# Three of six transformed rows of a 3x3 convolution by F(2,3) along the columns, and six half images' statistics by ScalarE's accumulators

## The chip, the cores and the metric

The kernel runs on one core of a Trainium2 chip. The metric is device time in microseconds (us) from the first to the last instruction of one execution; lower is better. Before the change it is 2940.79 us, the median of three runs from 2938.74 to 2942.02. The profile comes from one further execution with the hardware profiler on.

The engines are TensorE (PE, matmuls; PEld is its weight load, which overlaps), VectorE (DVE), ScalarE (ACT), GpSimd (POOL) and SyncE (SP, which issues DMAs). Each runs its own instructions in a fixed order; an instruction that waits holds up all that stand behind it on its engine. All data is float32.

## The reference

Two layers over `x` of shape (4, 1024, 56, 56). Layer 0 is a bottleneck with a deformable 3x3 convolution (bilinear samples at learned offsets). Layer 1 is a bottleneck with batch norms, whose means and variances run over all four images. The change lies for the most part in layer 1's 3x3 convolution and in the statistics of its output:

```python
x = relu(x + conv1x1(relu(deform_conv3x3(relu(conv1x1(x))))))            # layer 0
out = relu(bn(conv1x1(x, w1, b1), g1, be1))      # 1024 -> 256 channels
out = relu(bn(conv3x3(out, w2, b2), g2, be2))    # 256 -> 256, padding 1
out = bn(conv1x1(out, w3, b3), g3, be3)          # 256 -> 1024
x = relu(x + softplus(residual_scale)[0] * out)
```

## The kernel before

Channels lie on the 128 partitions, 256 of them as two blocks (KB = 2). The kernel has four stages, told apart here by their time in the profiled execution.

1. Layer 0 and layer 1's first 1x1 convolution, 0 to 2145 us. POOL gathers samples, ACT and DVE weight them, PE turns and multiplies them; positions (`stage_b`: o, oi, fl, hi, lo, each with two buffers) are worked out by DVE. In the last image, `filters()` transforms layer 1's 3x3 weights on DVE in pieces, one piece at two of nine taps, and `raw_rows` loads the first rows.
2. Layer 1's 3x3 convolution, 2145 to 2489 us. Below called the column stage.
3. The second norm with its ReLU (L977), and the third norm's statistics out of a matrix of second moments (L947, L966), up to about 2620 us.
4. The last 1x1 convolution, residual and output, to the end.

The column stage works on eight half images (`parts`), each 28 rows of 56 columns. Along the rows it is a Winograd transform F(4,3): groups of four output rows come out of six transformed rows p = 0 to 5 (`v[p]`, seven groups in a half image), with transformed filters `u[p]` that still have three column taps. Along the columns each transformed row is a filter of three taps. It is done with even and odd columns apart: `v[p]` holds the columns as two halves, `vs[p]` their difference, and `us[p]` is the sum of two taps. With these a row p takes five products in place of six. A product is four matmuls (two output blocks by two input blocks) of 196 columns (7 groups x 28), or 203 where one more column is needed; a matmul takes one 128x128 block of weights.

For a row p, `begin` issues eight matmuls into the bank `q` and four into `b`; ACT copies both out (L840, L841) into the rows `TARGET[p]` of the output `y2`, odd and even columns; DVE adds `b` to the odd ones (L844). `end` issues eight more matmuls into `q`, and DVE subtracts them from the even columns (L861). The rows are taken in the order `SEQ` = 1, 2, 3, 4, 0, 5. `end` of p = 2 and p = 4 also carries the inverse transform along the rows on DVE (L869 to L879, its last line writes row 1 of each group, which is the last reader of row 3 before p = 5 is copied there), `end` of 0 and 5 closes it (L883, L886), and `bn_stats` (L866) reads every finished row, eight times 392 elements in a half image.

The inputs of the next half image are made on the way: `load` takes the raw rows by DMA, and ACT normalizes them into one buffer `rows` (L744, four instructions of 784 to 812 elements), which DVE must have finished reading; the last reader is the input of p = 5 (L780, L781), the first user of the new rows is the input of p = 1 and 2 (L770 to L776). `inputs` computes `v[p]` and `vs[p]` (L783) on DVE.

The loop over (half image, p) issues `begin(i, p)`, then `end` of the row before, then inputs of the next half image, then `load` once for each half image. A scheduler may shift instructions on their engine from there, so the order is the one that stands in the built program.

PSUM has eight banks: three `q` of two banks, one `b` of two.

Of the kernel before, what the change touches and what calls it, by code (L numbers as in the profile page):

```python
# [8 lines left out]
F32 = mybir.dt.float32  # L9
I32 = mybir.dt.int32  # L10
AF = mybir.ActivationFunctionType
ALU = mybir.AluOpType
# [17 lines left out]
SEQ = (1, 2, 3, 4, 0, 5)  # L30
TARGET = (0, 0, 1, 2, 3, 3)

SIZES = (512, 512, 512, 512, 384, 384, 320)
# [25 lines left out]
def deform_bottleneck_then_bn_bottleneck(  # L59
# [48 lines left out]
    nc.vector.memset(eps_t, EPS)  # L108
    y1_stats = const.tile([128, KB, NB, 6], F32, tag="y1_stats", name="y1_stats")
    y2_stats = const.tile([128, KB, N * HW // PIECE, 6], F32, tag="y2_stats", name="y2_stats")  # L110

    def scale_shift(stats, k, g, be, name):

        mv = const.tile([128, k, 2], F32, tag=f"mv_{name}", name=f"mv_{name}")
        for i in range(k):
            nc.vector.bn_aggr(mv[:, i, :], stats[:, i, :, :].rearrange("p b s -> p (b s)"))
        return scale_shift_of(mv[:, :, 0], mv[:, :, 1], k, g, be, name)
# [43 lines left out]
    l1 = ExitStack()  # L161
    u, first_rows = [], []

    with ExitStack() as l0:
# [56 lines left out]

        zero = wp.tile([PW + 2, CB], F32, tag="zero", name="zero")
        nc.vector.memset(zero, 0.0)
        def load_zeros():
            for n in range(N):
                for corner, s in enumerate((0, PW)):
                    first_row = PW - s + TPAD
                    for r0, r1 in ((0, first_row), (first_row + H * PW, TROWS)):
                        if r1 > r0:
                            nc.sync.dma_start(tables[n][r0:r1, corner, :], zero[: r1 - r0, :])  # L230
# [109 lines left out]
        def stage_b(n, j):  # L340
# [16 lines left out]
            shape = [128, NT, TAPS, 2]  # L357
            o = work.tile(shape, F32, tag="o", name=f"o_{n}_{j}")[:, :nt]
            oi = work.tile(shape, I32, tag="oi", name=f"oi_{n}_{j}")[:, :nt]
            fl = work.tile(shape, F32, tag="fl", name=f"fl_{n}_{j}")[:, :nt]  # L360
            hi = work.tile(shape, F32, tag="hi", name=f"hi_{n}_{j}")[:, :nt]
            lo = work.tile(shape, F32, tag="lo", name=f"lo_{n}_{j}")[:, :nt]

# [102 lines left out]
        def stage_c(n, j):  # L466
# [56 lines left out]
            for h in range(KB):  # L523
                y1 = w3p.tile([128, 512], F32, tag="x1t", name=f"y1_{b}_{h}", bufs=X1S)
                y1 = y1[:, :size]
                nc.scalar.activation(y1, acc3[:, h, :size], AF.Identity, bias=col("b1", h))
                nc.vector.bn_stats(y1_stats[:, h, b, :], y1)
                nc.sync.dma_start(y1_v[n, :, h, blk], y1)
# [6 lines left out]
        def filters():  # L535
# [34 lines left out]
            yield  # L570
            nc.vector.tensor_scalar_mul(w_0, w_0, 0.25)
            yield

# [65 lines left out]
        for i, (n, j, k) in enumerate(taps):  # L639
# [10 lines left out]
            if (n, j, k) == (N - 1, 1, 0):  # L650
                l0a.close()
                extra = filters()
            if extra and k in (3, 7):
                next(extra, None)
# [28 lines left out]
    with l1:  # L683

        psq = l1.enter_context(tc.tile_pool(name="psq", bufs=3, space=bass.MemoryType.PSUM))
        psb = l1.enter_context(tc.tile_pool(name="psb", bufs=1, space=bass.MemoryType.PSUM))
        wino = l1.enter_context(tc.tile_pool(name="wino", bufs=1))

        stt = nc.vector.scalar_tensor_tensor


        v, vs = [], []
        for p in range(6):
            t = wino.tile([128, QUADS, KB, PW], F32, tag=f"v{p}", name=f"v{p}")
            for side in (0, PW - 1):
                nc.gpsimd.memset(t[:, :, :, side : side + 1], 0.0)
            v.append(t)
            vs.append(wino.tile([128, QUADS, KB, PW // 2], F32, tag=f"vs{p}", name=f"vs{p}"))

        us = [  # L700
            wino.tile([128, KB, CB], F32, tag=f"us{p}", name=f"us{p}") for p in range(6)
        ]
        sum_t = wino.tile([128, KB, QUADS, W], F32, tag="sum_t", name="sum_t")
# [49 lines left out]
        def inputs(i, d, ps):  # L753

            for hs in [slice(h, h + 1) for h in range(KB)] if i == 0 else [slice(0, KB)]:

# [7 lines left out]
                if len(ps) == 2:  # L764
                    p, q = ps
                    x = of(q)
                    y = wino.tile([128, QUADS, KB, W], F32, tag="y", name=f"y{p}_{i}_{hs.start}")
                    y = y[:, :, hs]
                    if p == 1:
# [7 lines left out]
                else:  # L777
# [3 lines left out]
                    stt(of(p), row(r), 4.0, of(p), ALU.mult, ALU.add)  # L781
                for p in ps:
                    stt(  # L783
                        vs[p][:, :, hs], v[p][:, :, hs, : PW // 2], -1.0, v[p][:, :, hs, PW // 2 :],
                        ALU.mult, ALU.subtract,
                    )


# [9 lines left out]

        def taps_of(ps, p, o, terms, start, stop):
            of = slice(o * 128, (o + 1) * 128)  # L800
            terms = [(wt[:, h, of], x[:, :, h]) for h in range(KB) for wt, x in terms]
            for i, (wt, x) in enumerate(terms):
                nc.tensor.matmul(  # L803
                    ps,
                    wt,
                    x,
                    start=start and i == 0,
                    stop=stop and i == len(terms) - 1,

                    skip_group_check=not (start and stop),  # L810
                )

        def cells(t, width):
            return t[:, :, : QUADS * width].rearrange("p o (r c) -> p o r c", c=width)

        def begin(i, p):

            n, half = parts[i]
            at = f"{p}_{i}"
            to = rows_of(n, half, TARGET[p])  # L820
            even, odd = to[:, :, :, 0:W:2], to[:, :, :, 1:W:2]
            x0, x1 = v[p][:, :, :, : PW // 2], v[p][:, :, :, PW // 2 :]
            pq = psq.tile([128, KB, 512], F32, tag="q", name=f"q{at}")
            for o in range(KB):
                taps_of(
                    pq[:, o, : QUADS * half_w], p, o,
                    [(u[p][:, :, c], x1[:, :, :, c // 2 : c // 2 + half_w]) for c in (0, 2)],
                    True, False,
                )
            pb = psb.tile([128, KB, 512], F32, tag="b", name=f"b{at}")  # L830
            for o in range(KB):
                taps_of(
                    pb[:, o, : QUADS * (half_w + 1)], p, o,
                    [(u[p][:, :, 1], x0)], True, True,
                )
            q, b = cells(pq, half_w), cells(pb, half_w + 1)
            for o in [slice(o, o + 1) for o in range(KB)] if p == 1 else [slice(0, KB)]:

                bias = col("b2", o.start) if p == 1 else 0.0
                nc.scalar.activation(odd[:, o], q[:, o], AF.Identity, bias=bias)  # L840
                nc.scalar.activation(  # L841
                    even[:, o], b[:, o, :, :half_w], AF.Identity, bias=bias, scale=-1.0
                )
            nc.vector.tensor_add(odd, odd, b[:, :, :, 1:])  # L844
            return pq

        def end(i, p, pq):

            n, half = parts[i]
            for o in range(KB):  # L850
                taps_of(
                    pq[:, o, : QUADS * half_w], p, o,
                    [
                        (us[p], vs[p][:, :, :, :half_w]),
                        (u[p][:, :, 2], vs[p][:, :, :, 1 : 1 + half_w]),
                    ],
                    False, True,
                )
            r = [rows_of(n, half, k) for k in range(4)]
            even = r[TARGET[p]][:, :, :, 0:W:2]  # L860
            nc.vector.tensor_sub(even, even, cells(pq, half_w))  # L861

            def stats(k):
                b = i * 4 + k
                for o in range(KB):
                    nc.vector.bn_stats(y2_stats[:, o, b, :], r[k][:, o])  # L866

# [17 lines left out]
            elif p == 5:  # L885
                nc.vector.tensor_add(r[3], r[3], far_t)  # L886
                stats(3)

        ds = {0: load(0)}
        for ps in ((1, 2), (3, 4), (0,), (5,)):  # L890
            inputs(0, ds[0], ps)
            for p in ps:
                nc.vector.tensor_add(us[p], u[p][:, :, 0], u[p][:, :, 1])
        before = None
        for i, p in [(i, p) for i in range(len(parts)) for p in SEQ] + [(len(parts), None)]:
            begun = begin(i, p) if p is not None else None
            if before is not None:
                j, q, _ = before
                end(*before)
                if j + 1 < len(parts) and q in (2, 4, 0, 5):  # L900
                    inputs(j + 1, ds[j + 1], (q - 1, q) if q in (2, 4) else (q,))
            if p == SEQ[0] and i + 1 < len(parts):
                ds[i + 1] = load(i + 1)
# [244 lines left out]
```

## Time and profile before

| | |
|---|---|
| median of three runs | 2940.79 us (2938.74 to 2942.02) |
| the profiled execution | 2943.16 us, its span 2941.3 us |
| PE busy | 2878.5 us (98%), 10665 matmuls |
| DVE busy | 1872.9 us (64%) |
| ACT busy | 1143.8 us (39%) |
| POOL busy | 1009.5 us (34%) |
| mean granted TensorE clock | 0.992 |

By stage, from the busy time of each engine in stretches of the span:

| stretch (us) | length | PE | DVE | ACT |
|---|---|---|---|---|
| 1900 to 2050, layer 0 | 150.0 | 150.00 | 103.26 | 64.45 |
| 2157 to 2486, column stage | 329.0 | 327.69 | 261.18 | 82.98 |
| 2486 to 2497, its end | 11.0 | 3.43 | 7.36 | 5.19 |
| 2497 to 2620, second moments | 123.0 | 123.00 | 46.85 | 41.74 |
| 2620 to 2941, output | 321.0 | 316.98 | 145.11 | 145.33 |

A mean duration counts one instruction from its start to its end. Two neighbours on DVE overlap by some 0.08 us where nothing is waited for, so the distance from start to start is shorter than the mean: 0.48 us for 392 elements whose mean is 0.56. Sums below use that distance.

### The profile page before, as it was taken

What the parts mean: (1) busy time and instruction counts of PE and PEld (TensorE: products, weight loads), DVE (VectorE), ACT (ScalarE), POOL (GpSimd) and SP (SyncE); (2) the same over time, 40 slices, a digit from 0 to 9 for tenths busy, and PEclk for the clock granted to TensorE, in tenths of its full rate; (3) what the DMA queues carried; (4) which work ended last, traced back from release to release, by engine and by line L of the source; (5) the groups of instructions that cost most, each with busy time, mean ns of one, the idle gap of its engine ahead of it and who ended that gap; (6) DMA issues with size and microseconds to landing.
All of it is one profiled execution on the core that took longest, in us unless ns stands there. A gap on an engine that the chain in (4) does not pass through costs nothing.

```text
span 2941.3 us, 34573 instructions
## 1 busy us (share of the span) xinstructions
PE 2878.5 (98%) x10665; PEld 1730.7 (59%) x10665; DVE 1872.9 (64%) x4234; ACT 1143.8 (39%) x2343; POOL 1009.5 (34%) x977
## 2 busy tenths in 40 slices
PE   8899999999999999999999899999989998999999
PEld 4444455565555555555555455455689998965554
DVE  2188666676666677566666867667477786344444
ACT  1144443444443444433433344444332222334444
POOL 0065554455455455454454654444100000000000
PEclk9999999999999999999999999999999999999999
DMA  7699999898998998989897899998521101049998
GB/s 250 198 375 382 329 328 321 298 354 319 325 339 313 342 288 336 333 323 343 324 322 268 319 336 330 333 320 299 184 75 46 46 23 54 25 148 316 303 308 263
DMA packets 330329, 789.48 MB, mean 268 GB/s; under 512 B 31352, under 2 KB 176800, under 8 KB 329888
## 3 DMA queue, kind: packets, MB, share of 16 engines
q0 software_dynamic: 127296, 462.48, 44.3%
q1 hardware_dynamic: 172368, 273.41, 27.7%
q10 hardware_dynamic: 30480, 51.39, 4.8%
q8 instruction: 84, 1.38, 0.2%
q14 instruction: 101, 0.83, 0.1%
HBM read 639.11 MB, written 142.70 MB: 266 GB/s over the span
## 4 chain that ended last, share of the span: by engine, by line
PE 90%; DMA 5%; DVE 2%; issue 1%; ACT 1%; SPq 0%; POOL 0%; DVEq 0%; ACTq 0%; POOLq 0%
PE acc L451 23%; PE pf L916 11%; PE acc L262 11%; PE pr L503 10%; PE acc L476 10%; PE q L803 9%; PE stp L435 6%; DMA g<-table,idxs 3%; PE acc_g L966 2%; PE b L803 2%; PE pm L288 2%; DVE s L413 2%; DMA xr<-in_x_dram 1%; PE ftp L318 1%; PE tp L947 1%
## 5 line engine op out<-in xcount | busy, mean ns | idle before, releaser
L401 POOL DMA_INDIRECT g<-table,idxs x900 | 1001.6, 1113 | 1086.7 <-DVE s L413 533.8
L413 DVE SCALAR_TENSOR_TENSOR s<-g,wts,s 128x256 f32<-128x256 f32 (+1 forms) x2700 | 1133.8, 479 | 353.1 <-ACT s L411 227.5
L451 PE MATMUL acc<-sts,w 128*128 128x512 f32 (+2 forms) x2016 | 809.8, 543 | 1.1 <-issue 0.8
L411 ACT ACTIVATE s<-g,wts 128x256 f32<-128x256 f32 x900 | 418.5, 509 | 459.6 <-PE stp L435 342.6
L451 PEld LDWEIGHTS acc<-sts,w 128*128 128x128 f32 x2016 | 363.1, 191 | 283.4 <-issue 201.1
L503 PE MATMUL pr<-r,w 128*128 128x512 f32 (+2 forms) x896 | 368.9, 543 | 7.1 <-ACT sts L441 3.5
L476 PE MATMUL acc<-x1t,c1w 128*128 128x512 f32 (+2 forms) x896 | 368.0, 539 | 5.2 <-ACT x1t L513 4.3
L262 PE MATMUL acc<-xt,w 128*128 128x448 f32 x896 | 354.5, 546 | 13.1 <-DMA xt<-in_x_dram 8.6
L916 PE MATMUL pf<-y,c3w 128*128 128x448 f32 x844 | 317.4, 539 | 0.0
L513 ACT ACTIVATE x1t<-x1t 128x512 f32<-128x512 f32 (+2 forms) x224 | 128.7, 575 | 439.2 <-DVE x1t L510 398.3
L435 PEld LDWEIGHTS stp<-ident,s 128*128 128x128 f32 (+1 forms) x1800 | 212.0, 141 | 138.9 <-issue 89.3
L510 DVE SCALAR_TENSOR_TENSOR x1t<-pr,ch,xr 128x512 f32<-128x512 f32 (+2 forms) x224 | 152.0, 681 | 214.7 <-PE pr L503 148.0
L262 PEld LDWEIGHTS acc<-xt,w 128*128 128x128 f32 x896 | 170.0, 192 | 173.0 <-issue 161.3
L476 PEld LDWEIGHTS acc<-x1t,c1w 128*128 128x128 f32 x896 | 170.0, 190 | 170.0 <-issue 117.7
L503 PEld LDWEIGHTS pr<-r,w 128*128 128x128 f32 x896 | 169.8, 191 | 165.9 <-issue 105.4
L441 ACT COPY sts<-stp 128x512 f32<-128x512 f32 (+2 forms) x504 | 243.1, 526 | 36.1 <-PE stp L435 22.1
L435 PE MATMUL stp<-ident,s 128*128 128x128 f32 (+1 forms) x1800 | 246.2, 273 | 9.9 <-DVE x1t L510 4.9
L1080 DVE SCALAR_TENSOR_TENSOR x1f<-pf,sc_bn,x1f 128x448 f32<-128x448 f32 x211 | 144.3, 684 | 172.3 <-PE pf L916 155.7
L916 PEld LDWEIGHTS pf<-y,c3w 128*128 128x128 f32 x844 | 160.4, 190 | 156.8 <-issue 118.4
L1088 ACT ACTIVATE x1f<-x1f,sh_bn 128x448 f32<-128x448 f32 x224 | 148.2, 667 | 173.8 <-DVE x1f L1080 172.1
L803 PE MATMUL q<-v,u 128*128 128x196 f32 x768 | 140.7, 335 | 9.6 <-DVE v L775 9.6
L803 PEld LDWEIGHTS q<-v,u 128*128 128x128 f32 x768 | 133.2, 191 | 10.5 <-ACT y L744 10.1
(174 smaller groups left out, 1713.3 us busy)
## 6 DMA issues: line engine op xcount, KB each, us to landing
xt<-in_x_dram SPq DMA_DIRECT2D x112, 448.0 KB
x1f<-x_d SPq DMA_DIRECT2D x112, 448.0 KB
out_dram<-x1f ACTq DMA_DIRECT2D x111, 448.0 KB
xr<-in_x_dram SPq DMA_DIRECT2D x64, 512.0 KB
x_d<-x1t SPq DMA_DIRECT2D x128, 256.0 KB
table<-ft SPq DMA_DIRECT2D x56, 384.0 KB
g<-table,idxs POOLq DMA_INDIRECT x900
xr<-in_x_dram SPq DMA_DIRECT2D x32, 384.0 KB
```

What stands on the lines that cost most here:

```text
L262: nc.tensor.matmul(acc[:, h, :BLK], w1[:, k, h * 128 : (h + 1) * 128], xt[:, k % 2, :], start=(k == 0), stop=(k == KC - 1),)
L401: nc.gpsimd.indirect_dma_start(out=g[:m], out_offset=None, in_=tables[n].rearrange("r q c -> r (q c)"), in_offset=bass.IndirectOffsetOnAxi ...
L411: nc.scalar.activation(s[:m], g[:m, 0:CB], AF.Copy, scale=wt[:, 0])
L413: nc.vector.scalar_tensor_tensor(s[:m], g[:m, corner * CB : (corner + 1) * CB], wt[:, corner], s[:m], ALU.mult, ALU.add,)
L435: nc.tensor.transpose(banks[h][:, t * 128 : t * 128 + m], s[:m, h * 128 : (h + 1) * 128], ident[:m, :m],)
L441: nc.scalar.copy(sts[:, h, :size], banks[h][:, :size])
L451: nc.tensor.matmul(acc[:, o, :size], w2[:, h, k, o * 128 : (o + 1) * 128], sts[:, h, :size], start=(k == 0 and h == 0), stop=(k == TAPS - ...
L476: nc.tensor.matmul(acc3[:, h, :size], c1w[:, k, h * 128 : (h + 1) * 128], x1t, start=(k == 0), stop=(k == KC - 1),)
L503: nc.tensor.matmul(pr, w3[:, h, k * 128 : (k + 1) * 128], r2[:, h, :size], start=(h == 0), stop=(h == KB - 1),)
L510: nc.vector.scalar_tensor_tensor(x1t, pr, col("a_b3", k), xr[:, d, :], ALU.add, ALU.add)
L803: nc.tensor.matmul(ps, wt, x, start=start and i == 0, stop=stop and i == len(terms) - 1,  skip_group_check=not (start and stop),)
L916: nc.tensor.matmul(pz, c3w[:, h, k * 128 : (k + 1) * 128], y2[n][:, h, j * BLK : (j + 1) * BLK], start=(h == 0), stop=(h == KB - 1),)
```

## The change

Rows p = 2, 4 and 5 (`WIN`) take another column transform: F(2,3), four products for two output columns. Its weights are made by `column_filters`: (w0 + w2 + w1)/2 goes over tap 1, (w0 + w2 - w1)/2 into `us[p]`; those of p = 2 and 4 (`EARLY`) are made in layer 0, as six more pieces of `filters()`, which now advances at three of nine taps. Its inputs take three DVE instructions for each p: a sum and a difference of the halves into `vs[p]`, now 56 columns wide, and a difference in place, whose column 0 POOL must have set to zero. `begin` now issues four matmuls into `q`, ACT copies -2 times that into the odd columns; a new step `middle` adds four more, and ACT copies the sum into the even columns; `end` adds four into `q` and four into a `b` of their own; DVE adds `q` to the odd and subtracts `b` from the even columns. `q` and `b` are one bank each, with four buffers each.

`bn_stats` stays for the first and the last half image. The six between are read by ACT (`passes`): two halves of each channel block, each with Identity and with Square, 784 elements, less the first half image's mean, with the sum from the accumulator; `gather` makes one entry of them for `bn_aggr`. The passes of a half image stand among the steps of the next one.

The intermediate `y` of `inputs` takes the place of `vs[q]`. The position tiles o, oi, fl, hi, lo have one buffer each; the zero tile for the tables' borders is taken from the ring of the samples' tiles.

```diff
+WIN = (2, 4, 5)
+EARLY = (2, 4)
...
-    y2_stats = const.tile([128, KB, N * HW // PIECE, 6], F32, tag="y2_stats", name="y2_stats")
+    y1_stats = const.tile([128, KB, NB * 6], F32, tag="y1_stats", name="y1_stats")
+
+    y2_stats = const.tile([128, KB, 3 + 2 * 4 * 6], F32, tag="y2_stats", name="y2_stats")
...
-            o = work.tile(shape, F32, tag="o", name=f"o_{n}_{j}")[:, :nt]
-            oi = work.tile(shape, I32, tag="oi", name=f"oi_{n}_{j}")[:, :nt]
-            fl = work.tile(shape, F32, tag="fl", name=f"fl_{n}_{j}")[:, :nt]
-            hi = work.tile(shape, F32, tag="hi", name=f"hi_{n}_{j}")[:, :nt]
-            lo = work.tile(shape, F32, tag="lo", name=f"lo_{n}_{j}")[:, :nt]
+            o = work.tile(shape, F32, tag="o", name=f"o_{n}_{j}", bufs=1)[:, :nt]
+            oi = work.tile(shape, I32, tag="oi", name=f"oi_{n}_{j}", bufs=1)[:, :nt]
+            fl = work.tile(shape, F32, tag="fl", name=f"fl_{n}_{j}", bufs=1)[:, :nt]
+            hi = work.tile(shape, F32, tag="hi", name=f"hi_{n}_{j}", bufs=1)[:, :nt]
+            lo = work.tile(shape, F32, tag="lo", name=f"lo_{n}_{j}", bufs=1)[:, :nt]
...
+            for p in EARLY:
+                us[p] = pool.tile([128, KB, CB], F32, tag=f"us{p}", name=f"us{p}")
+                yield from column_filters(p)
+
+        def column_filters(p):
+
+            w_0, w_1, w_2 = (u[p][:, :, j] for j in range(3))
+            nc.vector.tensor_add(us[p], w_0, w_2)
+            yield
+            nc.vector.tensor_add(w_1, w_1, us[p])
+            nc.vector.tensor_scalar_mul(w_1, w_1, 0.5)
+            yield
+            nc.vector.tensor_sub(us[p], us[p], w_1)
...
-            if extra and k in (3, 7):
+            if extra and k in (1, 4, 7):
...
-        psq = l1.enter_context(tc.tile_pool(name="psq", bufs=3, space=bass.MemoryType.PSUM))
-        psb = l1.enter_context(tc.tile_pool(name="psb", bufs=1, space=bass.MemoryType.PSUM))
+        psq = l1.enter_context(tc.tile_pool(name="psq", bufs=4, space=bass.MemoryType.PSUM))
+        psb = l1.enter_context(tc.tile_pool(name="psb", bufs=4, space=bass.MemoryType.PSUM))
...
+            half_c = PW // 2
+            for p in ps:
+                if p in WIN and i:
+                    nc.gpsimd.memset(v[p][:, :, :, 0:1], 0.0)
...
-                    y = wino.tile([128, QUADS, KB, W], F32, tag="y", name=f"y{p}_{i}_{hs.start}")
-                    y = y[:, :, hs]
+
+                    y = vs[q][:, :, hs]
...
+                    if p in WIN:
+                        x0, x1 = v[p][:, :, hs, 1:half_c], v[p][:, :, hs, half_c : 2 * half_c - 1]
+                        nc.vector.tensor_add(vs[p][:, :, hs, : W // 2], x1, x0)
+                        nc.vector.tensor_sub(vs[p][:, :, hs, W // 2 :], x0, x1)
+                        x = v[p][:, :, hs].rearrange("p r h (e c) -> p r h e c", e=2)
+                        to, nxt = x[..., : half_c - 1], x[..., 1:]
+                        nc.vector.tensor_sub(to, nxt, to)
+                        continue
...
+        def products(ps, terms, first=False, last=False, alone=False):
+
+            for o in range(KB):
+                of = slice(o * 128, (o + 1) * 128)
+                pairs = [(wt[:, h, of], x[:, :, h]) for h in range(KB) for wt, x in terms]
+                for j, (wt, x) in enumerate(pairs):
+                    nc.tensor.matmul(
+                        ps[:, o].rearrange("p r c -> p (r c)"),
+                        wt,
+                        x,
+                        start=first and j == 0 and (alone or o == 0),
+                        stop=last and j == len(pairs) - 1,
+                        skip_group_check=not alone,
...
+                products(q, [(us[p], vs[p][..., half_w:])], first=True)
+                nc.scalar.activation(odd, q, AF.Copy, scale=-2.0)
+                return q
...
+        def middle(i, p, q):
+            if p in WIN:
+                even, _ = halves(i, p)
+                products(q, [(u[p][:, :, 1], vs[p][..., :half_w])])
+                nc.scalar.copy(even, q)
...
+                x0, x1 = v[p][..., :half_w], v[p][..., PW // 2 : PW // 2 + half_w]
+                products(q, [(u[p][:, :, 2], x1)], last=True)
+                b = bank(psb, "b", i, p, half_w)
+                products(b, [(u[p][:, :, 0], x0)], first=True, last=True, alone=True)
+                nc.vector.tensor_add(odd, odd, q)
...
+                if i in ENDS:
+                    for o in range(KB):
+                        at = 3 + (ENDS.index(i) * 4 + k) * 6
+                        nc.vector.bn_stats(y2_stats[:, o, at : at + 6], r[k][:, o])
...
+        def passes(i):
+            n, half = parts[i]
+            size = HALF * W // CUTS
+            for o in range(KB):
+                for c in range(CUTS):
+                    at = half * HALF * W + c * size
+                    k = (i - 1) * CUTS + c
+                    for f, func in enumerate((AF.Identity, AF.Square)):
+                        nc.scalar.activation(
+                            passed,
+                            y2[n][:, o, at : at + size],
+                            func,
+                            bias=away[:, o : o + 1],
+                            accum_out=moved[:, f, o, k : k + 1],
+                        )
+                        yield
...
+        def gather():
+            count = float(between * HALF * W)
+            whole = y2_stats[:, :, 0:3]
+            nc.vector.tensor_reduce(in_sum, moved, mybir.AxisListType.X, ALU.add)
+            nc.vector.memset(whole[:, :, 0], count)
+            stt(whole[:, :, 1], in_sum[:, 0], 1.0 / count, mv_0[:, :, 0], ALU.mult, ALU.add)
+            nc.vector.tensor_mul(in_sum[:, 0], in_sum[:, 0], in_sum[:, 0])
+            stt(
+                whole[:, :, 2], in_sum[:, 0], -1.0 / count, in_sum[:, 1], ALU.mult, ALU.add
+            )
...
+                if q == SEQ[-1]:
+                    if j == 0:
+                        reference()
+                    elif j not in ENDS:
+                        passing = passes(j)
+                for _ in range(2):
+                    next(passing, None)
+                if (j, q) == (len(parts) - 1, SEQ[-2]):
+                    gather()
+            if p is not None:
+                middle(i, p, begun)
```

## The prediction

> **What bounds it now.** I read the page's busy line first, then the column stage half image by half image in the table of windows (in each line: the stretch, its length, then busy time and instructions of PE, PEld, DVE, ACT, POOL, the clock and the DMA), then its groups by shape, then the order of time.
>
> ```profile
> PE 2878.5 (98%) x10665; PEld 1730.7 (59%) x10665; DVE 1872.9 (64%) x4234; ACT 1143.8 (39%) x2343; POOL 1009.5 (34%) x977
> ...
> 2239.83:2280.72 40.89, 40.89 (x242) 40.67 (x241) 33.15 (x52) 10.56 (x19) 0.38 (x2) 1.00 0.13 41
> 2280.72:2321.61 40.89, 40.89 (x241) 40.68 (x241) 33.14 (x52) 12.00 (x23) 0.00 (x0) 1.00 0.13 41
> ```
>
> A half image takes 40.89 us, and PE has no gap in them; DVE works 33.1 of them, ACT 10.6 to 12. So matmuls are time here, DVE has 7.75 us to spare and ACT 29.
>
> ```profile
> L803 PE MATMUL b<-v,u 128*128 128x203 f32 x49 | 9.8, 337 | 0.0
> L866 DVE BATCH_NORM_STATS2 y_stats<-y 128x6 f32<-128x392 f32 x8 | 4.2, 560 | 0.0
> L744 ACT ACTIVATE rows<-y,sh_bn,sc_bn 128x784 f32<-128x784 f32 x4 | 4.1, 1095 | 2.1 <-issue 2.1
> L783 DVE SCALAR_TENSOR_TENSOR vs<-v 128x406 f32<-128x406 f32 x6 | 3.4, 575 | 0.0
> L773 DVE TENSOR_TENSOR v<-rows 128x784 f32<-128x784 f32 x1 | 1.0, 974 | 1.1 <-PE b L803 1.1
> ```
>
> These price what goes (203-column matmuls, bn_stats, the difference `vs`) and what comes (DVE on 784 elements, ACT on 784). Where the dependence lies shows in the order of time:
>
> ```profile
> 2243.28 0.97 DVE L781 SCALAR_TENSOR_TENSOR v<-rows,v 128x784 f32<-128x784 f32 x1
> ...
> 2244.33 4.10 ACT L744 ACTIVATE rows<-y,sh_bn,sc_bn 128x784 f32<-128x784 f32 x4 [2.15 <-issue]
> ...
> 2248.47 0.98 DVE L770 SCALAR_TENSOR_TENSOR v<-rows 128x784 f32<-128x784 f32 x1 [1.29 <-ACT rows L744]
> ```
>
> DVE frees `rows`, ACT refills them in 4.1 us, and DVE then waits 1.29 us for ACT. This loop goes round once in a half image, and the change puts work into it.
>
> **Matmuls removed.** A WIN row goes from 20 matmuls to 16; the four that go have 203 columns. In the chain of waits such four take 1.37 to 1.38 us, 0.344 each. 3 rows x 4 x 8 half images = 96 x 0.344 = **33.0 us**, and 40.89 becomes 36.76. If nothing else came in the way, that would be the gain.
>
> **DVE in a half image.** Removed: 3 x L783 (0.50 from start to start) = 1.5 and 8 bn_stats (0.48) = 3.9. Added: for each WIN row two of 392 elements (0.48) and one of 784 (L773: 0.97 long, 0.88 to 1.00 from start to start; 0.95) = 5.7. So 33.1 - 5.4 + 5.7 = 33.5 us in 36.76. The spare time falls from 7.75 to 3.3 us: what DVE waits beyond 3.3 us now lengthens the half image.
>
> **ACT in a half image.** Two copies for each row stay. Eight passes come in. No row of the trace has an accumulator; the nearest are L744 (784 elements, 1.10 long, 1.03 apart) and L977 (448 elements 0.75 and 128 elements 0.49 long, so 0.81 ns an element: 1.02 at 784). Reading the accumulator out has no row at all: 0, or as much as ACT's two-element Sqrt (L123, 0.30). I take **1.15 us** a pass, ends 0.95 and 1.35; 9.2 us, and ACT has 21 of 37 us filled. Here a rule speaks against the change: the Trainium skill, ScalarE: Activation LUTs, Rules for kernel authors, sends adds and multiplies to VectorE. By the rows it is right about the price: 9.2 us on ACT for 3.9 on DVE. Followed, bn_stats stay, DVE has 37.4 us of work, already above PE's 36.76, and with waits of some 2 us for `rows` (4.1 less the 2.4 behind them, below) a half image takes 39 to 40. With the passes DVE has 33.5, but what matters is where they stand in ACT's queue. The same table's price, 0.3 us and 0.83 ns an element, makes a pass 0.95: my lower end, since the row on 784 elements is longer. No table load comes in: the built program loads ACT's functions in the same three places as before.
>
> **The loop.** I walk one middle half image along the queues of the built program (the fourth to sixth differ little). Zero is where DVE ends L879's counterpart, which frees row 3. ACT's first copy of p = 5 ends at 0.6; `middle` of p = 5 (4 x 0.338) at 1.95; the second copy at 2.5; PE meanwhile runs three matmuls of another row, then the four of `end` until 4.3; DVE has other work until then and adds and subtracts at 4.4. Then come the input of p = 5 and row 3's closing: closed at 6.75, `rows` free at 7.7. ACT has in its queue a pass, one L744, a pass, three L744, a pass, the second copy of p = 2, a pass, two copies of p = 3. The first pass waits for the closing, so `rows` are full at 6.75 + 2 x 1.15 + 4.1, some 13.25 with the handovers. DVE has 2.4 us of work behind 7.7, then waits 3.2. It needs the copy of p = 2 next (14.95, a wait of 0.75), then those of p = 3 (17.1, a wait of 1.65). From there PE and ACT are ahead of it. Waits 0.1 + 3.2 + 0.75 + 1.65 = 5.7, work 33.5: **39.2 us**. DVE and ACT bind, PE idles 2.4 us. Four passes lie in the loop, so 0.1 us on a pass is 0.4 us here: 38.4 at 0.95, 40.0 at 1.35.
>
> **The stage summed**, from the end of L879 in one half image to the next.
> - First: before, DVE runs from 2151.1 to 2196.9 with 3.15 us of waits. WIN inputs of the first half image, in two pieces of 0.27 + 0.27 + 0.48 - 0.28 each, add 3 x 2 x 0.73 = 4.4; those of the second 1.4 up to here; weights 0.7, with two rows' made in layer 0; 3.9 us of other inputs stand behind this point in the new order, and the waits are filled: 2196.3.
> - Second: no passes, but bn_stats of the first half image and carried inputs: 38.5.
> - Third: passes, but more DVE work between freeing and first use: 37.5. Fourth to sixth: 39.2. Seventh: 37.3 (two inputs stand later). Together 2427.1; before 2196.9 + 6 x 40.89 = 2442.2.
> - Last: no inputs, PE binds: 0.6 and 75 matmuls, 26.1 us, then DVE's chain 7.3: 2460.5, where before it is 2482.8. ACT's first copy of p = 4, behind six passes, comes at 18.2, when PE wants it.
> - End: two bn_aggr over 192 elements (1.89) become two over 51 (0.5 by elements, I take 0.7); `middle` of p = 5 puts ACT, PE, ACT, PE in a row (4.0) where 3.8 passed. 8.35 against 9.34 to the first ReLU, which ran at 2492.1.
>
> **Gain 22.3 + 1.0 = 23 us.** `gather`'s five small DVE instructions (0.17 to 0.4) lie where DVE waits for PE in the last half image; uncovered 1.3.
>
> **Edits at nothing.** Weights of two rows in layer 0: eight DVE instructions, 4.2 us, where DVE is 103 of 150 us busy; uncovered 4. Position tiles single: DVE alone writes and reads them, in order; but an image's last block reads its PSUM bank some 15 DVE instructions later and holds one of four banks, 0 to 3 us an image. Zero tile: its writer moves behind another memset in the first us, under the first loads; at most 1. POOL's 20 memsets (0.19 each at L739) stand in an idle queue; 0, at most 0.2 each. `y` in `vs[q]`: PE's last read of it is `middle`, long over. Both output blocks in one bank: p = 1's split copies wait for both, 0.7 us, under four buffers. Of layer 0's slightly other order I make 0, between -2 and 3.
>
> Span 2941.3 - 23 = 2918.3; with what lies around the span (1.9) the profiled execution would be 2920, and the median stood 2.4 below it: **2918**.
>
> **Rivals.**
> - **PE stays the bound.** For it: 33.5 is under 36.76, and the order puts other rows' matmuls around `middle`. Against: DVE's waits for ACT. All 33.0 go: 2908.
> - **Worse, but faster.** PE too waits for a copy behind passes, 40 to 41 in five half images: the gain is 9 to 17, 2924 to 2932.
> - **Slower: ACT's queue.** Its price is the accumulator's read-out, which counts four times in each of five half images and six times ahead of p = 4's copy in the last: 26 us for each us on a pass. From 2.05 us a pass the gain of 23 is gone; at 2.4 it is 2950. For it: no row prices the read-out. Against: it would have to take 1 us, three L123.
> - **No change within 0.2%** (5.9 us, about what a measurement here can tell from nothing): a pass of 1.85 to 2.2, or half images near 42 by waits that I don't see.
>
> **Chances.** Forecast 0.58; PE bound 0.18; worse but faster 0.11; no change 0.07; slower 0.06. The range 2906 to 2934 holds the first three, the bounds of a pass (2914 to 2923) and layer 0's.
>
> **What would show it.** Middle half images of 38.5 to 40 us with PE 36.6 busy are the forecast; 36.8 without a gap the first rival. DVE busy 33.5; passes of 1.15; DVE's idle time ahead of the inputs of p = 1 and 2 put down to ACT `rows`, about 3 us. The first matmul still at 2154.5. I am wrong if layer 0 moves by over 3 us, or if PE waits more for ACT than DVE does.

## The result, and the profile after

The changed kernel takes **2914.65 us**, the median of four runs (2911.68 to 2925.49), where the kernel before takes 2940.37 beside it (four runs, 2938.74 to 2942.02): a ratio of 0.9919, 95% interval 0.9893 to 0.9945. The forecast was 2918. The profiled execution is the longest of the four, 2925.49 with a span of 2923.6; 2920 was forecast for it.

The busy line of the page, after:

```profile
PE 2852.8 (98%) x10473; PEld 1700.7 (58%) x10473; DVE 1884.1 (64%) x4257; ACT 1188.6 (41%) x2439; POOL 1029.2 (35%) x998
```

PE has 192 instructions fewer. A float32 matmul leaves two records, so these are the 96 matmuls of the forecast. Two middle half images in the table of windows, with the columns as before:

```profile
2279.81:2317.41 37.60, 37.48 (x218) 36.23 (x217) 32.73 (x49) 19.46 (x38) 0.38 (x3) 1.00 0.14 45
2317.41:2354.63 37.22, 36.90 (x217) 36.31 (x217) 32.64 (x51) 17.81 (x34) 0.56 (x4) 1.00 0.13 46
```

The figure after the length is PE's: it is busy for all but 0.1 and 0.3 us. The half image was forecast at 39.2 us with PE idle for 2.4 of them. DVE has 32.7 us of work (33.5 forecast) and waits 4.6 to 4.9.

The groups by shape, the first four of two middle half images, the last of the end of the column stage:

```profile
L845 PE MATMUL b<-v,u 128*128 128x203 f32 x48 | 9.2, 333 | 0.0
...
L956 ACT ACTIVATE passed<-y,away 128x784 f32<-128x784 f32 x16 | 15.1, 946 | 9.6 <-DVE y L929 4.7 <-DVE y L902 3.7 <-DVE y L894 1.2
...
L956 ACT ACTIVATION_READ_ACCUMULATOR passed<-y,away 128x1 f32 x16 | 3.1, 191 | 0.0
...
L793 DVE SCALAR_TENSOR_TENSOR vs<-rows 128x784 f32<-128x784 f32 x2 | 1.9, 973 | 2.8 <-ACT rows L762 2.8
...
L119 DVE BATCH_NORM_AGGREGATE mv_bn<-y_stats 128x2 f32<-128x51 f32 x2 | 0.6, 347 | 0.0
```

The 203-column records were 49 in one half image and are 24 now. The price that no row gave is here: a pass is an ACTIVATE of 0.946 us, and its accumulator is read by an instruction of its own, 0.191. DVE waits for the refilled `rows` (L762). The loop that the forecast walked, in order of time:

```profile
2325.27 0.97 DVE L803 SCALAR_TENSOR_TENSOR v<-rows,v 128x784 f32<-128x784 f32 x1
...
2326.24 0.18 ACT L956 ACTIVATION_READ_ACCUMULATOR passed<-y,away 128x1 f32 x1
2326.33 1.10 ACT L762 ACTIVATE rows<-y,sh_bn,sc_bn 128x784 f32<-128x784 f32 x1
2327.35 0.93 ACT L956 ACTIVATE passed<-y,away 128x784 f32<-128x784 f32 x1
...
2328.28 3.08 ACT L762 ACTIVATE rows<-y,sh_bn,sc_bn 128x784 f32<-128x784 f32 x3
...
2331.39 0.97 DVE L793 SCALAR_TENSOR_TENSOR vs<-rows 128x784 f32<-128x784 f32 x1 [2.65 <-ACT rows L762]
```

It runs as walked: DVE frees `rows` (L803), ACT refills them with a pass in between, and DVE waits 2.65 us (forecast 3.2). Behind a pass the next instruction starts 0.92 to 1.11 us after it, 0.99 in the mean and not 1.15: the read-out overlaps its neighbours.

**Where the time went.** I measure the column stage from its first `q` matmul to the first of `first` (L1089). It shrinks from 339.5 (2154.5 to 2493.96) to 310.5 us (2165.4 to 2475.86): 29.0. Cut at the start of L922, the last step of the row inverse (L879 before):

| piece | before | after | gain | forecast gain |
|---|---|---|---|---|
| first half image | 41.4 | 40.1 | 1.3 | 0.6 |
| six middle ones | 245.3 | 223.7 | 21.7 | 14.5 |
| the last | 40.5 | 33.8 | 6.7 | 7.2 |
| the end, to `first` | 12.2 | 12.9 | -0.7 | 1.0 |
| together | 339.5 | 310.5 | 29.0 | 23.3 |

In this execution layer 0 gives 10.9 us back: the column stage begins at 2165.4 and not at 2154.5. All of the experiments below look at one of these two figures: why the middle half images are 7 us shorter than forecast, and what layer 0 does.

### The profile page after: what moved, and what is told of

Same layout as the page of the kernel before. It is cut to its first block, busy times and chain, and to the rows that moved or that the text cites. A ratio compares the mean times of both kernels' runs of the same rounds, so it can differ in the third digit from the quotient of the medians.

```text
span 2923.6 us, 34375 instructions
## 1 busy us (share of the span) xinstructions
PE 2852.8 (98%) x10473; PEld 1700.7 (58%) x10473; DVE 1884.1 (64%) x4257; ACT 1188.6 (41%) x2439; POOL 1029.2 (35%) x998
## 5 line engine op out<-in xcount | busy, mean ns | idle before, releaser
L405 POOL DMA_INDIRECT g<-table,idxs x900 | 1018.3, 1131 | 1080.8 <-DVE s L417 550.9
L845 PE MATMUL q<-v,u 128*128 128x196 f32 x576 | 109.5, 337 | 10.9 <-DVE v L797 9.7
L845 PEld LDWEIGHTS q<-v,u 128*128 128x128 f32 x576 | 99.4, 191 | 15.6 <-ACT y L762 10.2
```

What stands on the lines that cost most here:

```text
L405: nc.gpsimd.indirect_dma_start(out=g[:m], out_offset=None, in_=tables[n].rearrange("r q c -> r (q c)"), in_offset=bass.IndirectOffsetOnAxi ...
L845: nc.tensor.matmul(ps[:, o].rearrange("p r c -> p (r c)"), wt, x, start=first and j == 0 and (alone or o == 0), stop=last and j == len(pai ...
```

## The experiments

In the expectations, theory M (in the first ones the rival) says that matmuls set a half image as long as DVE's work fits beside them; each row by F(2,3) takes 4 x 0.344 = 1.376 us of matmuls, so n rows make 40.89 - 1.376 n. Theory Q (the loop theory of the first ones) is the forecast's: waits for ACT's queue add to DVE's work. Each ratio is to the kernel before, measured beside: 2946.93 us (27 runs, 2932.62 to 2955.46) for the first four experiments, 2945.91 (7 runs) for the next four and 2943.09 (12 runs) for the last four. What the middle half images took:

| kernel | rows | six middle ones, mean | matmuls alone | stage | median |
|---|---|---|---|---|---|
| before | 0 | 40.89 | 40.89 | 339.5 | 2940.37 |
| before with the passes | 0 | 41.03 | 40.89 | 338.1 | 2941.57 (one run) |
| two rows | 2 | 38.14 | 38.14 | 316.3 | 2923.29 |
| changed | 3 | 37.28, 37.22, 37.29 | 36.76 | 310.5, 308.5, 310.9 | 2914.65, 2914.6, 2913.97 |
| changed, passes behind the loop | 3 | 37.05 | 36.76 | 311.3 | 2915.73 |
| changed, first half image by passes | 3 | 37.14 | 36.76 | 310.1 | 2914.7 |
| changed, all `bn_stats` | 3 | 36.80 | 36.76 | 309.2 | 2918.43 |
| four rows | 4 | 35.57, 35.58 | 35.39 | 301.3, 301.5 | 2907.91, 2903.43 |
| four rows, all `bn_stats` | 4 | 37.70 | 35.39 | 310.7 | 2911.97 |
| five rows | 5 | 38.71 | 34.01 | 325.3 | 2932.86 |

**The changed kernel again.**

> The changed kernel as it is. Column stage (first matmul of the stage to the first matmul behind the second norm): 310.5 us in the first profile. Both theories of it expect 310.5 +- 0.5 again. Layer 0 ended 10.9 us later than before in that profile, yet the medians are 25.7 us apart where the stage alone gives 29. Theory A (the edits in layer 0 cost time): the stage's first matmul again near 2165. Theory B (layer 0 scatters from run to run by the timing of its gathers, whatever the edits): another place between 2150 and 2165, total between 2911 and 2926 as that place moves.

Ratio 0.988 (0.9863 to 0.9897). The stage is 308.5 us, but begins at 2167.5, in an execution of 2925.92; the other three took 2910.8 to 2915.84. The stage repeats to some 2 us, and 1.4 of them lie at its end (below). Its start is again late, as theory A has it, in the longest of the four executions; the start moves on to 2156.0 in the third profile.

**All statistics back on DVE**, three rows kept.

```diff
-        ENDS = (0, len(parts) - 1)
+        ENDS = tuple(range(len(parts)))
...
-                if q == SEQ[-1]:
-                    if j == 0:
-                        reference()
-                    elif j not in ENDS:
-                        passing = passes(j)
-                for _ in range(2):
-                    next(passing, None)
```

> bn_stats on DVE for all eight half images, no passes on ACT, no gather; the columns' transform stays. Loop theory (DVE's work plus what it waits for ACT sets a middle half image): DVE's work 32.7 + 8 x 0.48 = 36.5, waits about 2, so 38 to 39 us instead of 37.2 to 37.6, and 1.2 us more at the end for bn_aggr: 8 to 12 us slower than the changed kernel. Rival (the number of matmuls alone sets it, statistics are hidden on either engine): 36.6 to 37.5 as before, at most 1.5 us slower.

The median is 2918.43 (ratio 0.9893, 0.9878 to 0.9908), the stage 309.2. Two of its middle half images in the table of windows:

```profile
2242.00:2316.00 74.00, 74.00 (x438) 73.34 (x437) 73.31 (x116) 22.86 (x40) 1.12 (x8) 1.00 0.14 46
```

And every wait of DVE in them, from the order of time:

```profile
2265.65 0.56 DVE L876 TENSOR_TENSOR y<-y,b 128x392 f32<-128x392 f32 x1 [0.18 <-ACT y L873]
2267.73 0.56 DVE L895 TENSOR_TENSOR y<-y,b 128x392 f32<-128x392 f32 x1 [0.16 <-PE b L845]
2302.28 0.56 DVE L876 TENSOR_TENSOR y<-y,b 128x392 f32<-128x392 f32 x1 [0.19 <-ACT y L873]
2304.36 0.56 DVE L895 TENSOR_TENSOR y<-y,b 128x392 f32<-128x392 f32 x1 [0.16 <-PE b L845]
```

DVE has 36.7 us of work in a half image and waits 0.35. Theory Q, by which waits of some 2 us for `rows` stay and make 39 to 40 us, is refuted: the added `bn_stats` fill the time in which DVE waited, and PE has no gap left. The run also takes the passes off ACT, so `rows` are refilled sooner; the runs with other numbers of rows leave them there. With three rows, moving the statistics to ACT gains nothing. It costs 0.5 us in each middle half image (37.3 against 36.8) and gives back the shorter `bn_aggr`.

**The passes behind the loop.** None is handed out at the step that closes a half image nor at the next row. In the queue as built one pass still stands ahead of the refill of `rows`.

```diff
-                for _ in range(2):
+                for _ in range(2 if q in (2, 3, 4, 0) else 0):
```

> The same eight passes, but none is handed out at the step that closes a half image nor at the first row of the next; two each at rows 2, 3, 4 and 0. Loop theory: of the four passes in the loop one stays ahead of the refill of rows; the wait of DVE for rows falls from 2.7 to about 1.8 us, those for the copies of rows 2 and 3 to under 0.5: a middle half image 36.6 to 36.9, PE bound, 3 us off the whole. Rival (a fixed cost of PE at the new step between two ACT copies, not the passes): no change within 1 us.

DVE's waits for `rows` from 2204 to 2430 us (in each line: us in total, times, the longest), first in the changed kernel, then here:

```profile
DVE vs L793 <- ACT rows L762: 8.2, 3, 2.8
...
DVE vs L793 <- ACT rows L762: 5.8, 3, 2.1
```

The wait for `rows` falls from 2.7 to 1.9 us, as the loop theory has it (1.8). Ratio 0.9887 (0.987 to 0.9905), stage 311.3. The middle half images are shorter by 0.2 us each (37.05, where the loop theory named 36.6 to 36.9), 1.3 together, and the end is longer by as much (14.2), so the stage gains nothing, as the rival has it. The loop doesn't set the time; at most it holds a part of the 0.5 us above the matmuls alone.

**The kernel before with the five position tiles single.**

```diff
-            o = work.tile(shape, F32, tag="o", name=f"o_{n}_{j}")[:, :nt]
+            o = work.tile(shape, F32, tag="o", name=f"o_{n}_{j}", bufs=1)[:, :nt]
...
```

> The kernel before, with the five position tiles single and nothing else. Theory A (layer 0's edits cost): layer 0 ends 3 to 11 us later than before, total slower by as much. Theory B (scatter): total within 2 us of before, and no PE wait that names the position tiles.

2943.12 us (22 runs) against 2946.93, ratio 0.9992 (0.9981 to 1.0004). Single tiles cost nothing, so they are not what delays layer 0. Its column stage, 339.2 us, is that of before.

**Two and four rows.** The number of rows alone, and four with every `bn_stats` on DVE.

```diff
-WIN = (2, 4, 5)
+WIN = (2, 4)
```

> The changed kernel with F(2,3) on two rows (2 and 4) in place of three. Compared by the column stage in the trace (first matmul of the stage to the first one behind the second norm; 310.5 us in the changed kernel), since layer 0 scatters by more than the difference. Theory M (PE's matmuls set a half image wherever DVE's work is below PE's): PE 38.0 a half image, DVE 31.3; middle half images 38.0 to 38.3, stage 317 to 319. Theory Q (waits between DVE and ACT keep a middle half image near 37.3, as now): 38.0 too, but since now 0.7 above PE's work a part of the added matmuls is free: stage 313 to 315.

```diff
-WIN = (2, 4, 5)
+WIN = (0, 2, 4, 5)
```

> F(2,3) on four rows (0, 2, 4, 5), statistics on ACT as in the changed kernel. PE's work 35.2 a half image, DVE's 32.7 + 1.4 = 34.1. Theory M: middle half images 35.2 to 36, the first one longer by 2.5 us (DVE is full there), the last one shorter by 1.4: stage 303 to 306. Theory Q: the waits stay, middle half images 37.3, stage 310 to 312.

> Four rows as the one before, but bn_stats on DVE for all half images and no passes. DVE's work 36.5 + 1.4 = 37.9 against 35.2 on PE. If DVE's work is a bound of its own: middle half images 37.9 to 38.5, stage 315 to 319, slower than with passes by 11 us or more; the passes pay only here. If DVE's work were hidden as with three rows: 35.2 to 36, stage 302 to 306.

Two rows: ratio 0.9926 (0.9898 to 0.9954). It decides nothing between the theories: the stage of 316.3 lies between what both named, and for the middle half images both named 38. These take 38.14, which is what matmuls alone make. Four rows: 0.9878 (0.9858 to 0.9899), stage 301.3, shorter than either theory named. The last five middle half images, in the changed kernel and with four rows:

```profile
2242.56:2429.16 186.60, 186.06 (x1084) 181.77 (x1084) 164.58 (x248) 93.85 (x182) 2.82 (x20) 1.00 0.11 37
...
2237.62:2412.84 175.22, 174.35 (x1019) 170.24 (x1018) 168.70 (x255) 94.96 (x181) 3.43 (x25) 1.00 0.12 39
```

With three rows DVE has 32.9 us of work in each and waits 4.4; with four it has 33.7 (34.1 expected) and waits 1.3, the passes standing in ACT's queue as before. So the waits did not stay, against theory Q. A middle pair with four rows:

```profile
2310.19:2341.89 31.70, 31.62 (x186) 30.85 (x185) 31.46 (x48) 19.07 (x37) 0.69 (x5) 1.00 0.17 55
2341.89:2381.18 39.29, 39.29 (x232) 38.45 (x231) 36.66 (x56) 19.02 (x35) 0.69 (x5) 1.00 0.13 42
```

The cut at L922 falls unevenly here, 31.7 and 39.3 by turns, so only the mean means something; PE has no gap of note in this pair. With `bn_stats` on DVE it looks otherwise:

```profile
2241.67:2279.12 37.45, 36.17 (x210) 34.80 (x209) 37.45 (x61) 11.88 (x22) 0.68 (x5) 1.00 0.14 47
2279.12:2316.55 37.43, 36.21 (x210) 34.80 (x209) 37.43 (x60) 10.80 (x18) 0.69 (x5) 1.00 0.13 44
```

Now DVE's figure, the third behind the length, is the full one: 37.45 us of 37.45. So DVE binds here, by its work alone and without a wait added. In the stage the passes are worth 9.4 us with four rows (310.7 against 301.3), less than the 11 or more expected. The totals don't tell the two apart (2911.97 and 2907.91, ratios 0.9877 and 0.9878).

**The first half image through the passes too**, the second as the reference of the mean.

```diff
-        ENDS = (0, len(parts) - 1)
+        ENDS = (1, len(parts) - 1)
...
-                    if j == 0:
+                    if j == ENDS[0]:
                         reference()
-                    elif j not in ENDS:
+                        passing = passes(0)
+                    elif j > 1 and j not in ENDS:
```

> Three rows; the half image whose statistics stay on DVE is the second, not the first, and ACT reads the first one during the third. In the first half image DVE is busy for 40.8 of 40.9 us, so 8 x 0.48 us less of it: first half image 3 to 3.9 us shorter; the second has DVE work 32.7 + 3.9 = 36.6, no longer than PE's; the third has 16 passes on ACT. Stage 306.5 to 308 if DVE binds the first half image; 310.5 if not.

```profile
2157.20:2197.59 40.39, 40.24 (x229) 39.75 (x230) 40.39 (x81) 11.67 (x22) 0.37 (x3) 0.96 0.13 43
```

Stage 310.1, ratio 0.9892 (0.9862 to 0.9921): no gain. The first half image still takes 40.4 us. DVE is full in it and has 81 instructions, as in the changed kernel, so other work stands where the `bn_stats` stood. But PE is full as well (40.24 us), at a granted clock of 0.96. In the changed kernel:

```profile
2165.40:2205.50 40.10, 40.00 (x221) 39.49 (x222) 39.99 (x81) 11.36 (x22) 0.59 (x2) 0.93 0.13 44
```

Which of the two binds the first half image is not shown.

**The kernel before with the passes alone**, no row by F(2,3).

> The kernel before with nothing changed but the statistics: six half images through ScalarE's accumulators, no F(2,3) row. Theory M (matmuls set a half image as long as VectorE's work is shorter): the middle half images stay at 40.9, the stage from the first q matmul to the first of first is 338 to 339 (before 339.5; the smaller bn_aggr give 1.3 at the end, gather costs some of it), VectorE is busy 29.3 of 40.9. Rival Q (passes in ScalarE's queue delay copies that PE and VectorE wait for, whatever the bound): 41.3 to 41.5 a half image, as the passes seem to cost 0.5 in the changed kernel, and a stage of 341 to 343.

```profile
2235.06:2440.27 205.21, 204.84 (x1202) 203.34 (x1201) 148.68 (x216) 93.98 (x178) 0.96 (x5) 1.00 0.10 33
```

In these five half images DVE works 148.7 us, where five of before take 5 x 33.14 = 165.7, and the time stays: 41.03 a half image, 0.1 above theory M's figure and below the rival's. The stage of 338.1 is M's. The total is one run. The passes alone bring no time while PE is full.

**Five rows.**

```diff
-WIN = (2, 4, 5)
+WIN = (0, 2, 3, 4, 5)
...
-        passed = wino.tile([128, HALF * W // CUTS], F32, tag="passed", name="passed")
+        passed = wino.tile([128, HALF * W // CUTS], mybir.dt.bfloat16, tag="passed", name="passed")
```

> Five rows by F(2,3) (0, 2, 3, 4, 5); the tile that the passes write, which nobody reads, is of two bytes an element to make room. Matmuls alone: 40.89 - 5 x 1.376 = 34.0 a half image. VectorE's work: 31.5 with two rows, 32.9 with three, 33.7 with four, so 34.8 with five. Theory M: VectorE is now the longest, middle half images of 34.8 to 35.3, its busy share 99%; the first half image, where VectorE is full already, grows by 1 to 2; stage 297 to 300 (four rows 301.3), so the fifth row brings 2 to 4 us where each before brought 6 to 9. Rival Q (waits for ScalarE add to VectorE's work): 37 or more, stage above 310. Rival R (each row brings its matmuls, 11 us): stage 290 to 292.

A miss for theory M: the stage is 325.3 us, in rival Q's range and 24 longer than with four rows, and the total 2932.86 (ratio 0.9948, 0.9929 to 0.9966). Two half images:

```profile
2277.26:2319.01 41.75, 36.48 (x199) 34.44 (x198) 37.71 (x57) 18.86 (x34) 0.81 (x6) 0.92 0.12 39
2319.01:2352.89 33.88, 33.88 (x201) 33.13 (x200) 33.30 (x51) 19.58 (x38) 0.81 (x6) 1.00 0.15 52
```

No engine is full in the first. PE in it, in order of time:

```profile
2292.92 3.02 PE L845 MATMUL q<-vs,us 128*128 128x196 f32 x16 [0.36 <-DVE y L902]
2300.76 1.69 PE L845 MATMUL b<-v,u 128*128 128x203 f32 x4 [4.82 <-DVE v L797]
2302.48 2.81 PE L845 MATMUL q<-v,u 128*128 128x196 f32 x8
2305.13 1.49 PE L845 MATMUL q<-vs,u 128*128 128x196 f32 x8
```

PE has nothing left and waits 4.82 us for an input (L797), which stands on DVE behind the first steps of the row inverse. When it comes, eight records take 2.81 us and not 1.49, the granted clock of the half image is 0.92, and DVE then waits for PE in turn (0.90 us ahead of L894). In the six middle half images together, beside the same of four rows with every `bn_stats` on DVE (first line):

```profile
2204.24:2430.45 226.21, 217.46 (x1252) 209.13 (x1251) 224.76 (x355) 67.80 (x120) 4.09 (x30) 1.00 0.11 37
...
2203.26:2435.51 232.25, 212.99 (x1187) 202.84 (x1187) 217.07 (x331) 106.51 (x200) 4.87 (x36) 0.96 0.11 36
```

DVE's work is 36.2 us a half image in the mean of the six (35.5 in the last five, where 34.8 was expected), so it is now above PE's 34.0; and DVE waits 2.5 on top. Here work and waits add, to theory Q's size. But DVE being the longer one is not enough for that: in the first line it has 37.5 us of work against PE's 35.4, and it waits 0.2. There PE pauses by 1.1 to 1.8 us and the matmuls behind keep their pace (1.59 us for eight records); here its longest pauses are 4.82, 4.62 and 3.28 us, and each time the matmuls behind them take longer. It also has the passes in ACT's queue, which the first line has not, and DVE waits for ACT too (1.05 us ahead of L895 in the half image above). Which of these makes the waits add was not separated, and which rows, or which order, would avoid it was not tried. The two-byte tile is not it: a pass takes 0.947 us as before.

**Four rows and the changed kernel, side by side.**

> Four rows again, beside the changed kernel and before in the same runs. Theory M: stage 301 to 302, total 7 to 9 below the changed kernel and 33 to 38 below before, a ratio near 0.988. Rival (the first four-row run was luck of layer 0's scatter): the stage as short, but the totals overlap with the changed kernel's.

> The changed kernel, unchanged, in the same runs as four and five rows. Stage 308.5 to 310.5 in its trace, total 2911 to 2918, ratio 0.990 to 0.992; layer 0 ends anywhere between 2155 and 2168.

Four rows: **2903.43 us** (2897.49 to 2912.24), ratio to before 0.9865 (0.9844 to 0.9885), stage 301.5. Changed: 2913.97 (2913.16 to 2916.56), ratio 0.9901 (0.9886 to 0.9917), stage 310.9 (308.5 to 310.5 expected). The ranges don't overlap, and the 10.5 us between the medians, where 7 to 9 were expected, are the 9.4 of the stage and 1.1 that no view places. Four rows with the passes beat both kernels.

## Why the prediction was right in its size and wrong in a step

- **Matmuls removed, 33.0 us, PE full before.** Right. Each row takes 1.376 us a half image until DVE is nearly full.
- **The bound of a middle half image.** This step failed: "5.7 us of waits, 33.5 of work: 39.2; DVE and ACT bind, PE idles 2.4 us". The waits were found at the places named, L793 for `rows` first of all. But a wait of an engine with time to spare is not a term of a sum. It is where the spare time sits while PE works on. Measured are 37.3 us with PE idle for 0.1 to 0.3, near the 36.76 of the matmuls alone. Two runs show it. With `bn_stats` on DVE, 3.9 us more work came with as much less waiting. With four rows, the passes in ACT's queue as before, DVE waits 1.3 us and not 4.4: the matmuls went, and the waits shrank with them. Two terms were also mis-sized on the same side: DVE's work (32.7) and the pass (about 1.0 us, so 0.6 less for the four in the loop). With five rows, where DVE's work is above PE's, waits and work did add; with four rows and all `bn_stats`, where it is too, they did not.
- **The rule against the change.** The Trainium skill, ScalarE: Activation LUTs, Rules for kernel authors, sends adds and multiplies to VectorE. On the price it holds here: eight passes take ACT about 8 us (0.99 each) for 3.9 on DVE. The forecast made 39 to 40 us of following it; measured are 36.8, less than the 37.3 of not following it, and stages that can't be told apart (309.2 against 308.5 to 310.9). With four rows it turns round in the stage, 310.7 with the rule and 301.3 against it. The rule compares the two engines; which one has time to spare decides.
- **PE stays the bound**, the first rival, was nearer to the truth than the forecast: 37.3 against its 36.76. Its 33.0 us are 4.0 more than the stage gives: the first half image gains 1.3 and not 4.1 (PE and DVE are both full in it), the six middle ones 21.7 and not 24.8, the last 6.7 and not 4.1, and the end loses 0.7.
- **The end.** `middle` of p = 5 puts ACT, PE, ACT, PE in a row, 4.0 us by forecast. The order of time, after:

```profile
2464.09 0.52 ACT L859 ACTIVATE y<-q 128x392 f32<-128x392 f32 x1 [9.66 <-DVE y L922]
...
2464.66 2.98 PE L845 MATMUL q<-vs,u 128*128 128x196 f32 x8 [2.71 <-ACT y L859]
...
2467.68 0.51 ACT L883 COPY y<-q 128x392 f32<-128x392 f32 x1 [3.07 <-PE q L845]
...
2468.24 1.63 PE L845 MATMUL q<-v,u 128*128 128x196 f32 x8 [0.60 <-ACT y L883]
...
2469.91 0.56 DVE L894 TENSOR_TENSOR y<-y,q 128x392 f32<-128x392 f32 x1 [0.18 <-PE q L845]
```

  From L922's end at 2464.0 to L894 it takes 5.9 us, where 3.8 passed before: the first eight records, after PE stood still for 2.71 us, take 2.98 and the next eight 1.63. In the changed kernel again the same steps take 4.5 us, since after the same pause the first eight take 1.59:

```profile
2466.24 1.59 PE L845 MATMUL q<-vs,u 128*128 128x196 f32 x8 [2.72 <-ACT y L859]
2468.43 1.63 PE L845 MATMUL q<-v,u 128*128 128x196 f32 x8 [0.60 <-ACT y L883]
```

  There the end gains 0.7 us (12.2 to 11.5), near the 1.0 of the forecast; the loss of 0.7 in the first profile is the slow matmuls. `bn_aggr` gave its 1.28 back as forecast (1.89 to 0.61).

- **Layer 0, made 0, between -2 and 3.** In the profiled execution it is 10.9 us, outside. The changed kernel's three profiles begin the column stage at 2165.4, 2167.5 and 2156.0; the kernel before and its two variants at 2154.5, 2149.0 and 2154.6. All eleven profiles of kernels with the edits of layer 0 begin it at 2156.0 to 2167.5. So the profiled executions lie later. The medians don't show it: they gain 25.7, 32.3 and 29.1 us in the three comparisons of the changed kernel, the stage 29.0, 30.9 and 28.6. Single tiles alone cost nothing; the weights' earlier pieces were not tried alone. What delays the profiled executions stays open.

That 2918 came within 3.4 us of 2914.65 is therefore in part luck: the forecast had the stage 5.7 us too long, and in the median of that comparison some 3 us of the stage's gain are missing outside it. The sign, and that PE would remain nearly full, needed only the windows.

## What to carry to other kernels

When the engine that binds loses work, compare the next one's busy time with what is left, not its busy time plus its waits: waits of an engine with slack fill up when work comes, as long as the binding engine has queued work to go on with. Move work to an idle engine when the giver has become the bound: here the passes cost 3 us of middle half images with three rows and bring 9 us of the stage with four, though the totals don't show those 9. And stop while the engine that takes work on still has less of it than the one that is relieved: with four rows DVE had 33.7 us of work in a half image for PE's 35.4, the fifth row made it 35.5 for 34.0, and the stage lost 24 us where the fourth had gained 9.

## What the hardware showed that was not expected

- Reading an accumulator is an instruction of its own on ACT, 0.191 us behind an ACTIVATE of 0.946 on 784 elements; they overlap, and from the start of a pass to the next instruction's it takes 0.92 to 1.11.
- A pause of PE of some 2.7 us can go either way. In the three profiles of the changed kernel it is 2.71, 2.72 and 2.71 us ahead of the end, and the eight records behind it take 2.98, 1.59 and 2.98. With four rows they take 2.75 after 2.77. After 1.30 us in the kernel before, and after 2.35 with four rows and all `bn_stats`, they take 1.62 and 1.59. The Trainium skill, TensorE: Matmul & The Clock Gate, Why this matters for your kernels, puts the longest harmless pause near 3 us; here shorter ones were harmful in some executions.
- Executions of the same kernel before spread over 2932.62 to 2955.46 us on one chip, 0.8%, so a change of 3 us needs many runs or a look at its own stage. The stage has its own scatter, 2.4 us in three profiles of the changed kernel.
